# The last normalisation of a batch moves from VectorE to ScalarE, in a two-layer graph network kernel run from step lists

## The chip, the core and the metric

The kernel runs on one core of a Trainium2 chip. The core's engines each work through a queue of their own: TensorE (PE in the profile; PEld is its weight load), VectorE (DVE), ScalarE (ACT), GpSimd (POOL), and SyncE (SP), whose queue issues nearly all DMAs. They meet only at semaphores. The metric is the device time in microseconds of one execution; lower is better.

## The reference

Everything is float32. For each of 128 batches there are 128 agents with 512 features and an adjacency matrix. Layer 0 is attention with 8 heads, masked by the adjacency, and layer 1 a graph attention; each is followed by a residual and a layer norm.

```python
# layer 0
q, k, v = (x @ W + b for W, b in ((Wq, bq), (Wk, bk), (Wv, bv)))
logits = where(adj > 0, einsum('bqhd,bkhd->bhqk', q, k) / sqrt(64), -1e9)
out = relu(einsum('bhqk,bkhd->bqhd', softmax(logits), v) @ Wo + bo)
x = layernorm(x + out)
# layer 1
Wh = x @ W
e = where(adj > 0, leaky((Wh @ a1)[:, :, None] + (Wh @ a2)[:, None, :]), -9e15)
out = leaky(einsum('bij,bjf->bif', softmax(e, axis=1), Wh))
x = layernorm(x + out)            # the result: 128 x 128 x 512
```

`layernorm` is `(x - mean) / sqrt(var + 1e-5)` over the 512 features, without learned scale or offset. The normalisation that the change touches is the one in the last line.

## The kernel before

Four batches make a group. The products with Wq, Wk and Wv are made for a group at a time by Strassen's scheme, twice nested. Each of the three has two chains (numbered 0 to 5 within a group: Q, Q, K, K, V, V), and a chain has seven steps p1 to p7. A step in an even chain has 4 matrix products of 128x128x128, in an odd chain 3; the profile shows two MATMUL records for each, so 8 and 6. This document calls them group steps and writes "3.4's p2" for step p2 of chain 4 of group 3. The products with Wo (layer 0's output, `LayerZero`) and with layer 1's W (`LayerOne`) are made for pairs of batches, with seven products of 4 records each.

Each engine runs its instructions in the order in which the program emits them. That order is written out: `BEGIN` holds the tokens for the first six batches, `PLAN` those for the end, and `STEADY` has four lists, for batch t with t % 4 = 0, 1, 2, 3. A loop over t from 6 to 123 walks through the lists. An even t starts a pair and works on `LayerOne` of an earlier pair; an odd t works on `LayerZero` of the pair before. A token is a job and a method:

- `f` and `s`: softmax of the pair's first and second batch. `scores` are TensorE's (L872), `add` and `reduce` VectorE's (L886, L895), `exp` and `divide` ScalarE's, one instruction a head (L906, L920). Then `store` writes the weights to DRAM (L927), `fetch` reads them back in 4 pieces by blocks of 32 (L933), `transpose` turns them on VectorE (L939), and `attend` is TensorE's product with V (L952).
- `w`: layer 1's product of a pair (p1 to p7, L798), `z`: layer 0's output of a pair; `g`: normalised rows of layer 0 on the way back through DRAM, `g.transpose` turns them (L423); `p.sum`, `s.sum`, `m.sum`: sums of blocks on GpSimd.
- `e`: edge attention of one batch: `turn_blocks`, `add`, `maxima`, `exp`, `divide`, `product` (L1207), `copy` (L1214). `v`: its senders, through DRAM (L1248, L1258).
- `n`: the end of the batch before. `residual` (L1217), `stats` (L1000, L1002), `rstd` (GpSimd, L1006 and L1008), `apply`, `store` (L1230).
- `h`: the next group step on TensorE. `a` and `d`: the next of its reads of PSUM on ScalarE and VectorE. `k`: the next addition of a chain's blocks on GpSimd, `k.v` the same on VectorE (L728). `i.s1a` to `i.s4b`: inner sums of the features (L497), on GpSimd, or with `.v` on VectorE. `q`: the next load of weights on SP's queue (L631), into a ring of 4 buffers. `m`: loads, masks and turns of the inputs; `m.x_one` and `m.x_pair` load features (L418).

The norm's `apply` has two forms:

```python
if self.on_scalar:
    nc.scalar.activation(self.src, self.src, AF.Identity, bias=self.shift, scale=self.r)
    return
nc.vector.tensor_scalar(
    self.src, self.src, self.mv[:, 0:1], self.r, ALU.subtract, ALU.mult)
```

Before the change the steady lists use the second (L1021). The first (L1017) is used in PLAN alone, for 8 of the last 12 results (that of batch 116 and seven more) and for six rows of layer 0; there `rstd` makes the offset by two GpSimd instructions (L1011, L1013). PSUM gives five banks to scores, products and attention values in turn, and three to the group steps.

Of the kernel before, what the change touches and what calls it, by code (L numbers as in the profile page):

```python
# [8 lines left out]
F32 = mybir.dt.float32  # L9
# [3 lines left out]
ALU = mybir.AluOpType  # L13
# [56 lines left out]

STEADY = {
    0: """
        m.masks m.sum.0 f.scores m.sum.1 m.sum.2 k.v m.turn n.residual k.v g.apply.0
        s.scores w.p1 g.store.0 q g.fetch_both w.p5 f.add.1 f.add.0 f.reduce s.add.0 s.add.1
        e.turn_blocks q w.t0 w.p6 h q m.residuals f.exp.2.3 f.exp.0.1 h w.p2 h w.t2 e.add
        f.reciprocals.0 f.exp.4.5 f.exp.6.7 a d n.stats f.reciprocals.1 w.c11 e.maxima d
        w.p7 f.divide.0.1 f.divide.6.7 a w.t3 e.exp s.reduce h h f.divide.2.3 a f.divide.4.5
        m.sum.3 n.rstd e.divide i.s1b.v d w.c22 n.apply i.s1a w.p4 h n.store f.store s.exp.2
        w.c21 m.cast v.senders h s.exp.5 a v.store w.p3 s.exp.0.1 s.exp.3.4 h h e.product
        i.s2a.v k.v g.transpose.0 g.transpose.1 s.reciprocals.0 m.x_pair k f.fetch v.fetch a  # L80
        s.exp.6.7 s.divide.2 d m.mask i.s3a.v w.c12 d i.s2b e.copy i.s3b.v
    """,
    1: """
        z.by m.cast n.residual z.p2 s.reciprocals.1 k.v n.stats p.sum.0 i.s4a h h h z.p1 h a
        a d k.v h s.divide.0.1 s.divide.3.4 s.divide.5.6 s.divide.7 z.t0 h z.p6 z.bw a z.t2
        m.turn k.v h d f.transpose z.c11 e.turn_blocks z.p7 a z.p5 d z.t3 z.c22 s.store z.p4
        q e.add k k e.maxima m.mask s.fetch z.p3 h h p.sum.1 i.s4b n.rstd h n.apply e.exp a
        e.divide z.c12 z.c21 a e.product h z.stats.1 d n.store f.attend q q m.x_one
        s.transpose z.rstd.1 p.sum.2 s.attend z.stats.0 e.copy k.v z.apply.1 f.copy z.rstd.0
        s.copy s.sum.0 k k s.sum.2 p.sum.3 s.sum.1 z.store.1 s.sum.3  # L90
    """,
    2: """
        n.residual f.scores g.apply.0 e.turn_blocks s.scores w.p1 e.add w.p2 f.add.1 f.add.0
        e.maxima f.reduce w.t0 e.exp g.store.0 m.masks q m.residuals w.p6 f.exp.6.7 w.p5
        w.t2 f.exp.4.5 f.exp.0.1 w.p7 n.stats m.turn k.v f.reciprocals.1 k.v k.v w.c11 w.t3
        h h f.exp.2.3 a w.p4 f.reciprocals.0 w.c22 d h h f.divide.4.5 n.rstd n.apply
        e.divide w.c21 v.senders g.fetch_both m.x_one n.store w.p3 f.divide.6.7 s.add.0 a d
        s.add.1 g.transpose.1 w.c12 s.reduce g.transpose.0 h e.product h f.divide.2.3 m.cast
        f.divide.0.1 a a h h v.store q f.store e.copy d m.mask v.fetch
    """,  # L100
    3: """
        m.turn n.residual k.v k z.by z.bw s.exp.3.4 a z.p1 h s.exp.2 s.exp.5 z.t0 s.exp.0.1
        s.exp.6.7 d n.stats e.turn_blocks s.reciprocals.1 q h z.p6 a d s.reciprocals.0 h
        z.p5 h z.t2 s.divide.5.6 s.divide.7 h z.p7 s.divide.0.1 s.divide.3.4 f.fetch d
        f.transpose s.divide.2 a a q q s.store q q h m.cast z.t3 e.add h z.p4 h a k p.sum.0
        n.rstd p.sum.2 h z.p2 z.c22 k n.apply k.v d z.c21 e.maxima h z.p3 a e.exp a z.c11 d
        z.stats.1 e.divide z.c12 h h e.product h h s.fetch f.attend n.store k p.sum.1 k
        z.rstd.1 d z.apply.1 q q z.store.1 q m.x_one z.stats.0 s.transpose s.attend a e.copy
        f.copy s.copy a k k z.rstd.0 s.sum.0 p.sum.3 s.sum.2 s.sum.1 m.mask s.sum.3
    """,  # L110
}

# [53 lines left out]
def kernel(  # L166
# [18 lines left out]
    nc = tc.nc  # L185
    B, P, D = x.shape
# [9 lines left out]
    small = ctx.enter_context(tc.tile_pool(name="small", bufs=3))  # L196
# [795 lines left out]
    class Norm:  # L992


        def __init__(self, src, on_scalar=False):
            self.src, self.on_scalar = src, on_scalar

        def stats(self):
            st = small.tile([P, 6], F32, name="st", bufs=4)
            nc.vector.bn_stats(st, self.src)  # L1000
            self.mv = small.tile([P, 2], F32, name="mv", bufs=4)
            nc.vector.bn_aggr(self.mv, st)  # L1002

        def rstd(self):
            ve = small.tile([P, 1], F32, name="ve", bufs=4)
            nc.gpsimd.tensor_scalar_add(ve, self.mv[:, 1:2], EPS)  # L1006
            self.r = small.tile([P, 1], F32, name="rstd", bufs=4)
            nc.gpsimd.tensor_tensor(self.r, ve, mhalf, ALU.pow)  # L1008
            if self.on_scalar:
                minus = small.tile([P, 1], F32, name="minus", bufs=4)  # L1010
                nc.gpsimd.tensor_scalar_mul(minus, self.mv[:, 0:1], -1.0)  # L1011
                self.shift = small.tile([P, 1], F32, name="shift", bufs=4)
                nc.gpsimd.tensor_tensor(self.shift, minus, self.r, ALU.mult)  # L1013

        def apply(self):
            if self.on_scalar:
                nc.scalar.activation(  # L1017
                    self.src, self.src, AF.Identity, bias=self.shift, scale=self.r
                )
                return  # L1020
            nc.vector.tensor_scalar(  # L1021
                self.src, self.src, self.mv[:, 0:1], self.r, ALU.subtract, ALU.mult
            )
# [129 lines left out]
    class Edge:  # L1153
# [12 lines left out]
        e = None  # L1166
# [55 lines left out]

        def rstd(self):
            self.norm.rstd()

        def apply(self):
            self.norm.apply()
# [295 lines left out]
    for token in BEGIN.split():  # L1523
        if token[0] in "ig" and token[1] in "12":
            g = int(token[1])
# [44 lines left out]
    for t in range(6, END):  # L1570
# [11 lines left out]
        g = (t + 3) // GROUP  # L1582
# [169 lines left out]
```

## Time and profile before

| what | value |
|---|---|
| median of 3 runs | 2266.84 us (2261.54 to 2272.79) |
| the profiled execution, its own time | 2263.41 us |
| its span, first to last instruction | 2261.6 us |
| granted TensorE clock | 0.998 |
| PE, PEld, DVE, ACT, POOL busy | 2236.6, 2015.0, 2014.3, 1661.6, 1406.2 us |
| DMA | 540.78 MB, mean 239 GB/s |

The span has three stages: BEGIN until about 132 us, the loop with the STEADY lists until about 2142 us, and PLAN. In a row of the profile the columns are line, engine, operation, output<-input with shapes, count, then busy time in us and the mean of one in ns, then the idle time before them and what ended it. In a row of the chain of waits the columns are start, length and what ran. TensorE's ends are modelled, so the distance between starts is read for its steps.

### The profile page before, as it was taken

What the parts mean: (1) busy time and instruction counts of PE and PEld (TensorE: products, weight loads), DVE (VectorE), ACT (ScalarE), POOL (GpSimd) and SP (SyncE); (2) the same over time, 40 slices, a digit from 0 to 9 for tenths busy, and PEclk for the clock granted to TensorE, in tenths of its full rate; (3) what the DMA queues carried; (4) which work ended last, traced back from release to release, by engine and by line L of the source; (5) the groups of instructions that cost most, each with busy time, mean ns of one, the idle gap of its engine ahead of it and who ended that gap; (6) DMA issues with size and microseconds to landing.
All of it is one profiled execution on the core that took longest, in us unless ns stands there. A gap on an engine that the chain in (4) does not pass through costs nothing.

```text
span 2261.6 us, 52550 instructions
## 1 busy us (share of the span) xinstructions
PE 2236.6 (99%) x17228; PEld 2015.0 (89%) x17228; DVE 2014.3 (89%) x4225; ACT 1661.6 (73%) x5955; POOL 1406.2 (62%) x1697
## 2 busy tenths in 40 slices
PE   9899999999999999999999999999999999999998
PEld 6889999999999999999899999999999999999985
DVE  5889999999988999988999889999899988899977
ACT  3668777677677787776776777877767767778786
POOL 2666666656766566666567665666665676556656
PEclk9999999999999999999999999999999999999999
DMA  9988788887888888888888888888888888888764
GB/s 230 273 238 239 237 245 248 240 249 231 243 244 250 247 239 239 241 247 242 235 237 245 241 249 246 239 239 246 244 241 247 235 243 239 250 247 237 219 214 151
DMA packets 516592, 540.78 MB, mean 239 GB/s; under 512 B 100568, under 2 KB 394336, under 8 KB 516320
## 3 DMA queue, kind: packets, MB, share of 16 engines
q1 hardware_dynamic: 516000, 537.17, 81.3%
q8 instruction: 137, 2.24, 0.4%
q14 instruction: 135, 1.11, 0.2%
q10 hardware_dynamic: 320, 0.26, 0.0%
HBM read 388.96 MB, written 148.31 MB: 238 GB/s over the span
## 4 chain that ended last, share of the span: by engine, by line
PE 89%; DMA 4%; DVE 4%; ACT 1%; SPq 1%; issue 1%; POOL 0%; POOLq 0%; DVEq 0%; ACTq 0%
PE st_y L678 24%; PE p_y L798 19%; PE st_w L678 12%; PE p_w L798 9%; PE st_x L678 6%; PE lg L872 6%; PE p_oT L952 5%; PE p_x L798 5%; PE p_h L1207 4%; DMA adj<-in_adj_dram 1%; DMA paz<-pa_dram 1%; DMA w_n<-wv 0%; SPq L933 0%; ACT pa L920 0%; DVE pa L939 0%
## 5 line engine op out<-in xcount | busy, mean ns | idle before, releaser
L906 ACT ACTIVATE pa<-pa,nmax 128x128 f32<-128x128 f32 x1000 | 391.8, 397 | 11.7 <-DVE nmax L895 9.4
L920 ACT ACTIVATE pa<-pa,rs 128x128 f32<-128x128 f32 x1000 | 327.2, 401 | 4.1 <-DVE rs L916 4.1
L728 POOL TENSOR_TENSOR out_Q<-out_Q,cells 128x512 f32<-128x512 f32 x92 | 116.2, 1277 | 297.4 <-DVE out_Q L728 297.4
L691 ACT COPY cells<-st_y 128x384 f32<-128x384 f32 x279 | 133.0, 477 | 102.6 <-PE st_y L678 101.9
L967 ACT ACTIVATE arena<-p_oT,b_cols 128x128 f32<-128x128 f32 x504 | 138.1, 382 | 80.6 <-PE p_oT L952 79.7
L906 ACT ACTIVATION_READ_ACCUMULATOR pa<-pa,nmax 128x1 f32 x1000 | 193.4, 193 | 0.0
L1008 POOL TENSOR_TENSOR rstd<-ve,mhalf 128x1 f32<-128x1 f32 x256 | 161.4, 631 | 21.3
L1000 DVE BATCH_NORM_STATS2 st<-arena 128x6 f32<-128x512 f32 x248 | 168.8, 681 | 1.2
L1006 POOL TENSOR_SCALAR ve<-mv 128x1 f32<-128x1 f32 x256 | 76.1, 297 | 147.7 <-DVE mv L1002 145.0
L886 DVE TENSOR_TENSOR pa<-lg,mf 128x512 f32<-128x512 f32 x250 | 161.5, 675 | 3.7 <-PE lg L872 3.7
L939 DVE STREAM_TRANSPOSE pa<-paz 128x1024 f32<-128x1024 f32 x125 | 154.6, 1236 | 7.0 <-DMA w_n<-wv 3.0
L895 DVE TENSOR_REDUCE nmax<-pa 128x8 f32<-128x1024 f32 x125 | 151.0, 1208 | 1.2
L872 PE MATMUL lg<-out_K,out_Q 64*128 64x128 f32 x2048 | 139.6, 281 | 0.7 <-ACT out_K L1391 0.7
L872 PEld LDWEIGHTS lg<-out_K,out_Q 64*128 64x128 f32 x2048 | 125.2, 187 | 14.3 <-issue 7.2
L728 POOL TENSOR_TENSOR out_K<-out_K 128x512 f32<-128x512 f32 x62 | 79.1, 1275 | 91.1 <-DVE out_K L728 91.1
L712 DVE TENSOR_TENSOR cells<-st_w,cells 128x384 f32<-128x384 f32 (+1 forms) x217 | 120.9, 557 | 16.6 <-ACT cells L691 16.3
L798 PE MATMUL p_y<-wo_w,x1T 128*128 128x257 f32 x496 | 134.2, 393 | 0.0
L1214 ACT ACTIVATE arena<-p_h 128x512 f32<-128x512 f32 x120 | 71.9, 599 | 83.8 <-DMA out_dram<-arena 60.2
L798 PE MATMUL p_y<-wo_w,arena 128*128 128x256 f32 x504 | 131.3, 383 | 0.9 <-ACT pr_t L809 0.9
L1021 DVE TENSOR_SCALAR arena<-arena,mv,rstd 128x512 f32<-128x512 f32 x239 | 131.2, 549 | 0.6 <-POOL rstd L1008 0.6
L798 PE MATMUL p_y<-wo_w,oS 128*128 128x256 f32 x504 | 129.8, 380 | 0.1
L798 PE MATMUL p_y<-wo_w,x1S 128*128 128x257 f32 x496 | 128.2, 380 | 0.2 <-ACT arena L809 0.2
(301 smaller groups left out, 7720.8 us busy)
## 6 DMA issues: line engine op xcount, KB each, us to landing
paz<-pa_dram SPq DMA_DIRECT2D x504, 128.0 KB, 3.6
pa_dram<-pa SPq DMA_DIRECT2D x125, 512.0 KB, 3.8
w_n<-wk SPq DMA_DIRECT2D x93, 512.0 KB, 4.3
w_n<-wv SPq DMA_DIRECT2D x93, 512.0 KB, 5.1
w_n<-wk SPq DMA_DIRECT2D x93, 384.0 KB, 4.3
w_n<-wv SPq DMA_DIRECT2D x93, 384.0 KB, 3.5
x_dram<-arena SPq DMA_DIRECT2D x128, 256.0 KB, 2.6
xz<-x_dram SPq DMA_DIRECT2D x240, 128.0 KB, 3.8
```

Source lines behind the costliest of these rows:

```text
L678: nc.tensor.matmul(p[:, index, :], lhs, rhs, start=start and index == 0, stop=True, skip_group_check=True,)
L728: (by or engine).tensor_add(*(t(n) for t, n in (dst, left, right)))
L798: nc.tensor.matmul(p[:, :width], xs()[n][:, kc, :], w[:, PLACE[n], kc, :], start=start and kc == 0, stop=True, skip_group_check=True,)
L872: nc.tensor.matmul(self.lg[r][:, c, :], q[rows, 2 * (b % 2) + c % 2, c // 2, :], k[rows, 2 * (b % 2) + c % 2, c // 2, :], start=c == 0, st ...
L886: nc.vector.tensor_add(by_head[:, r * NC : (r + 1) * NC], self.lg[r].rearrange("p c (b k) -> p c b k", b=4), mf.unsqueeze(1).to_broadcast( ...
L895: nc.vector.tensor_reduce(self.nmax, by_head, AX.XY, ALU.max, negate=True)
L906: nc.scalar.activation(self.pa[:, :, h, :], self.pa[:, :, h, :], AF.Exp, bias=self.nmax[:, h : h + 1], accum_out=self.sums[:, h : h + 1],)
L920: nc.scalar.activation(self.pa[:, :, h, :], self.pa[:, :, h, :], AF.Copy, scale=self.rs[:, h : h + 1])
L939: nc.vector.transpose(self.paT.rearrange("p h (a i) -> p a h i", i=32), self.paz.rearrange("p a (h k) -> p a h k", k=32),)
L967: nc.scalar.activation(OT[pair][:, c, h * P : (h + 1) * P], self.oT[:, c, :], AF.Identity, bias=b_cols[:, 1, c : c + 1],)
L1000: nc.vector.bn_stats(st, self.src)
L1008: nc.gpsimd.tensor_tensor(self.r, ve, mhalf, ALU.pow)
```

## The change

`Edge` gets a token `move`. It makes the offset, -mean x rstd, by one VectorE instruction on 128x1 values and sets `on_scalar`, so that the `apply` which follows is ScalarE's. As `on_scalar` is set after `rstd` has run, GpSimd's two offset instructions are not emitted. All four STEADY lists have `n.move` added and are reordered throughout; BEGIN and PLAN are the same text.

```diff
+        def move(self):
+
+            self.shift = small.tile([P, 1], F32, name="shift", bufs=4)
+            nc.vector.scalar_tensor_tensor(
+                self.shift, self.mv[:, 0:1], -1.0, self.r, op0=ALU.mult, op1=ALU.mult
+            )
+            self.on_scalar = True
...
+        def move(self):
+            self.norm.move()
```

Of the lists, the parts that the prediction speaks of. The new list 0, from its start and around the weights' way:

```
m.sum.0 m.sum.1 m.sum.2 e.turn_blocks m.turn f.scores k.v n.residual m.masks k.v
g.apply.0 q f.add.0 f.add.1 s.scores w.p1 f.reduce a e.add w.t0 m.cast n.stats
m.mask g.store.0 n.rstd h f.exp.4.5 f.exp.2.3 m.sum.3 e.maxima w.p6 w.t2 f.exp.0.1
s.add.0 d s.add.1 f.reciprocals.0 h q m.residuals g.fetch_both a e.exp f.exp.6.7
f.divide.0.1 d s.reduce f.reciprocals.1 q q q w.p2 w.p7 h h w.p5 h a w.t3 a s.exp.5
f.divide.6.7 w.p4 n.move w.c22 i.s1b.v d w.c11 w.p3 h h e.divide g.transpose.1
g.transpose.0 n.apply f.divide.2.3 i.s1a w.c21 v.senders f.divide.4.5 n.store
s.exp.6.7 a v.store f.store h e.product h s.exp.3.4 s.exp.0.1 s.exp.2 a d k.v
m.x_pair i.s3b.v s.reciprocals.0 s.reciprocals.1 w.c12 d v.fetch i.s2a e.copy
f.fetch i.s3a i.s2b
```

The old list 0 from e.divide on:

```
e.divide i.s1b.v d w.c22 n.apply i.s1a w.p4 h n.store f.store s.exp.2
w.c21 m.cast v.senders h s.exp.5 a v.store w.p3 s.exp.0.1 s.exp.3.4 h h e.product
i.s2a.v k.v g.transpose.0 g.transpose.1 s.reciprocals.0 m.x_pair k f.fetch v.fetch a
s.exp.6.7 s.divide.2 d m.mask i.s3a.v w.c12 d i.s2b e.copy i.s3b.v
```

The new list 1:

```
z.p2 k p.sum.0 p.sum.2 h h s.divide.3.4 z.by a h z.p1 h h h n.residual n.stats k.v a
d s.divide.2 s.divide.0.1 s.divide.7 s.divide.5.6 k.v m.turn e.turn_blocks z.bw z.t0
a k.v z.p6 z.t2 z.p5 i.s4b k z.p7 n.rstd k i.s4a h f.transpose n.move s.store d z.t3
e.add e.maxima z.c22 a e.exp m.cast n.apply z.p4 h z.c21 e.divide h z.p3 d z.c11
z.stats.1 z.c12 q s.fetch h h e.product a a n.store d s.transpose z.stats.0 f.attend
z.rstd.1 q s.attend z.apply.1 e.copy p.sum.1 k k m.x_one f.copy s.copy z.rstd.0
s.sum.0 s.sum.2 s.sum.1 p.sum.3 k s.sum.3 m.mask z.store.1
```

Counted over the four lists, `h` goes from 9, 11, 8, 14 to 9, 11, 5, 17 (lists 0 to 3) and `q` from 3, 3, 2, 8 to 5, 2, 2, 7; `i.s2a` and `i.s3a` lose their `.v`; of the additions 13 instead of 12 are GpSimd's and 11 instead of 12 VectorE's.

## The prediction

> **What bounds the kernel now.** I read the page's busy line first, then busy time by stage, TensorE's waits, and the chain that ended last inside the steady stage.
>
> ```profile
> PE 2236.6 (99%) x17228; PEld 2015.0 (89%) x17228; DVE 2014.3 (89%) x4225; ACT 1661.6 (73%) x5955; POOL 1406.2 (62%) x1697
> ```
>
> ```profile
> 0.00:132.00 132.00, 121.08 (x777) 95.15 (x777) 96.50 (x186) 72.42 (x248) 69.38 (x67) 0.99 0.89 245
> 132.00:2142.00 2010.00, 2007.50 (x15767) 1830.64 (x15764) 1825.16 (x3828) 1497.72 (x5404) 1265.87 (x1512) 1.00 0.83 242
> 2142.00:2262.00 120.00, 108.06 (x690) 89.19 (x688) 92.66 (x213) 91.50 (x305) 70.97 (x120) 0.98 0.59 184
> ```
>
> The columns are PE, PEld, DVE, ACT, POOL, clock, DMA. The second row is the loop that uses the changed lists: TensorE (PE) idles 2.5 of 2010 us, VectorE (DVE) 185. The first and third rows are BEGIN and PLAN, which the change leaves alone; they hold 22.8 of the 25 us that TensorE idles.
>
> A busy TensorE could still be a slow one, so I looked at the length of its steps:
>
> ```profile
> 236.61 2.29 PE lg L872 x31
> ```
>
> ```profile
> 253.82 1.56 PE st_y L678 x14
> 260.46 0.89 PE st_y L678 x8
> 264.85 1.56 PE st_y L678 x14
> 267.30 0.86 PE p_h L1207 x2
> 268.83 1.90 PE p_oT L952 x32
> 270.73 1.99 PE lg L872 x32
> 272.71 1.06 PE p_y L798 x4
> ```
>
> 1.56/14 and 0.89/8 are both 0.111 us a matmul: a group step of 8 or 6 matmuls takes 0.89 or 0.67, wherever it stands. Only the scores (lg) differ: 1.99 in list 2, up to 2.29 in list 0. Starts of the scores of successive pairs are 34.90 and 34.08 us apart, 68.98 for four batches. The rows give: 21 steps of 8 and 21 of 6, 32.8; 28 products of 0.866, 24.2, and 0.2 more for each of the two behind the scores, 0.4; 4 products of 0.86, 3.4; attention values and scores of two pairs, 2x1.90 + 2x1.99 = 7.8. Sum 68.6. So one round of four lists has 0.3 to 0.4 us of give, some 10 us in the 29.5 rounds.
>
> Here a rule of the Trainium skill is weighed: "Perfetto Trace Analysis", section "Identifying the Most-Contended Engine", says that matmul busy time is a bad measure of TensorE's headroom and that LDWEIGHTS' busy share is a good one. By that rule 89% leaves 11%, 247 us, to be won. By the equal steps it is 10 us in the lists. I take the steps: nothing but the waits between them can go.
>
> **The change part by part.**
>
> The apply. 116 steady results (128 less the last 12, whose norm lies in PLAN) go from VectorE to ScalarE (ACT):
>
> ```profile
> L1021 DVE TENSOR_SCALAR arena<-arena,mv,rstd 128x512 f32<-128x512 f32 x239 | 131.2, 549 | 0.6 <-POOL rstd L1008 0.6
> L1017 ACT ACTIVATE arena<-arena,shift,rstd 128x512 f32<-128x512 f32 x9 | 7.3, 813 | 2.5 <-POOL shift L1013 2.3
> L1201 DVE RECIPROCAL rt<-total 128x1 f32<-128x1 f32 x128 | 19.6, 153 | 6.5 <-ACT att L1197 4.8 <-ACT wq L1197 1.5
> ```
>
> VectorE loses 116 x 0.549 = 63.7 us. The new offset instruction is 128x1; the trace has no 128x1 scalar_tensor_tensor. Nearest are this reciprocal (0.153) and the 128x2 aggregate L1002 (0.182); the 128x1 additions L394 had a median of 0.278, in a stage with queueing. I take 0.18: 20.9 us, between 18 and 32. ScalarE gains 116 x 0.813 = 94.3 us. The rule that speaks against this is in "ScalarE: Activation LUTs", section "Rules for kernel authors": additions and multiplications belong on VectorE, not ScalarE. Were both engines in series with TensorE, it would make the change 116 x (0.813 + 0.18 - 0.549) = +51.5 us. In the trace neither is: ScalarE has 512 us free in the loop. I put the direct cost at 0; the cover is TensorE's 68.6 us a round against about 51 of ScalarE, and if it failed wholly the price would be those 51.5.
>
> The lists. I summed each engine's instructions per round, each at the distance between starts that the trace shows when it runs back to back. VectorE goes from 61.3 to 58.2 us: apply and offset, and two sums of features (i.s2a, i.s3a: rows of 0.678 and 1.279, L497) that go to GpSimd. ScalarE goes from 48.7 to 51.5. GpSimd (POOL) goes from 42.1 to 45.3: it takes the two sums at 1.80 and 1.28. All stay under 68.6. On the page I expect VectorE near 1915 us, ScalarE 1755, GpSimd 1495, and TensorE unchanged: it has the same steps, the group steps in the same order among themselves; list 2 has 5 group steps instead of 8 and list 3 has 17 instead of 14. The DMAs are the same ones; only their places in the SP queue move. By themselves these moves cost 0: every sum stays covered.
>
> What a new order can win. In list 0 the second scores wait: K's last addition (k.v, L728) ran 236.82 to 237.50 on VectorE and the scores could have begun at 237.53; with their semaphore instructions they started at 237.64. The blocks of scores in list 0 are 0.14 to 0.48 over the 1.99 (mean 0.24), 7.3 us in all. In the new lists VectorE ends s's turn 1.7 us before list 0 begins (in list 3 its last waits are for p3 of 3.3, 4.6 us ahead; then 0.47 + 0.59 + 1.16 and what stood before); the turned edges 0.23, an addition 0.59, the residual 0.60 and K's last addition 0.59 then end 0.3 us into the list, 0.7 before the second scores at 0.99. Part of the 0.24 is the sequencer's own work, so I count -5 us (bounds 0 and -7). Short stalls at 1074 to 1094 cost 2.4 us once; with VectorE freer I count -1.
>
> What it can cost: queues. Places in a list are TensorE's steps added up from its first scores: w.p3 of the new list 0 ends at 2 scores 1.99 + 7 products 6.06 + 4 group steps of 8 and one of 6, 4.24 = 12.3. n.store waits in SP's queue for the apply on ScalarE; behind it stand v.store and f.store in lists 0 and 2, weight loads (q) and z.store in 1 and 3. ScalarE has the apply, some 0.72 at back-to-back spacing, ahead of two divisions of f in list 0. There five q now come before n.store; the last waits for a weight buffer that the Q/K/V step p3 frees at 10.6 us into the list, before the apply ends at 11.3: 0. n.move waits for GpSimd's rstd and holds VectorE's queue (w.c22, i.s1b, an addition). rstd stands behind three feature sums of 1.24; the first began 4.9 us into the old list 0, so rstd ends at 4.9 + 3.7 + 0.8 = 9.4. The first TensorE step that reads a bank which the held addition must empty (3.5's p2) starts at 13.65, the addition ends by 11.3: room of 2 us. On GpSimd list 1 has 17.0 us of work in 17.8; i.s4a, the last sum before the second Q chain, ends at 25.4 from list 0's start (i.s4b from 19.3: 0.96, two V additions of 1.24, rstd 0.82, i.s4a 1.83), its reader starts at 26.9: room of 1.5. The tightest place is list 1's turn:
>
> ```profile
> 249.79 0.38 SPq L927 DMA_DIRECT2D pa_dram<-pa  x1
> 252.13 1.82 SPq L418 DMA_DIRECT2D xz<-in_x_dram  x4
> 254.04 2.58 SPq L933 DMA_DIRECT2D paz<-pa_dram  x4
> 256.66 2.02 SPq L1258 DMA_DIRECT2D ez<-e_dram  x4
> ```
>
> ```profile
> 260.99 1.23 DVE L939 STREAM_TRANSPOSE pa<-paz 128x1024 f32<-128x1024 f32 x1
> 268.18 1.23 DVE L939 STREAM_TRANSPOSE pa<-paz 128x1024 f32<-128x1024 f32 x1
> ```
>
> The weights of head block f are stored (L927), fetched (L933) and turned (L939) on VectorE, then those of s; s is used by the second half of the 268.83 row, at 269.78, and turned at 269.41. Room: 0.37 us. In the new order the x loads (L418) can go 1.7 us earlier (their buffers are freed after w.p3, which ends 12.3 us into the list instead of 14.0), but v.fetch (L1258, 2.02 us of issue) now stands before f.fetch. So f.fetch begins about 0.3 us later, +17.8 instead of +17.5 into list 0, its last piece is down 6.4 to 6.8 us later (24.2 to 24.6), and VectorE, which had no idle time before this turn, waits for it some 1.6 us. From there to the end of s's turn the new list has 8.2 us on VectorE (the old one took 8.42): 32.4 to 32.8. The s product starts at 32.69. I put half of the win back: +2.
>
> Sum against the profiled execution's own time, 2263.4 (span 2261.6 and 1.8 around it): -5 - 1 + 2 = -4, 2259.4. The median shown, 2266.84, lies 3.4 above that execution, so I round up to 2260.
>
> **The rivals.**
>
> Slower: a late turn in list 1. Each 0.1 us that f's fetch lands later than 24.6 delays s's product by as much, 29 times: 2.9 us. It decides from 0.6 us: 18 us, 2278; at 1 us it gives 29 us, 2289. For it: the room above is nil by my sums, n.apply stands ahead of f.store and v.store, and v.fetch must wait for v.store's landing (3.0 us before). Against it: the x loads come earlier, and VectorE's own share is shorter.
>
> No change: TensorE's 68.6 us a round hid everything before and hides it now; the waits at the scores only change place. 2263 to 2267.
>
> Faster by more: all of the list's give and most of the small stalls go, and executions like the slower two of the three shown had more such stalls, which a freer VectorE absorbs. 2261.6 + 1.8 - 7.3 - 2.5 = 2253.6; nothing in the lists can give more.
>
> Doing nothing is not possible for the instructions, but it is for the time: that is the second case.
>
> **How the numbers follow.** 0.5% is 11.3 us, about what a measurement of this kernel can tell from no change: below 2255.5 is faster, above 2278.2 slower. The forecast (2255.5 to 2266) has 0.38, no change 0.08, the late turn 0.30 (0.05 of it too small to count as slower), more gain 0.18, all of it below 2255.5, other new waits, in an order whose rooms are about 0.5 us, 0.06 (slower). So faster 0.18, same 0.38 + 0.08 + 0.05 = 0.51, slower 0.25 + 0.06 = 0.31. The range takes in most of the larger gain, to 2252, and the late turn up to 0.9 us, 2286; some 0.05 lies below and 0.1 above.
>
> **What would show it.** Right: TensorE's loop still within 3 us of full, VectorE's share near 85%, ScalarE's near 78%, scores of list 0 at 2.0 to 2.1 us, 116 more applies on ScalarE at about 0.81 us. Wrong: idle time of TensorE at p_oT ended by VectorE's turn (L939) and the turn idle until DMA paz, above 0.3 us in every fourth list; or group steps (L678) waiting for VectorE's additions. A time outside 2252 to 2286 or a TensorE with fewer idle microseconds in BEGIN and PLAN would mean that I read the bound wrongly.

## The result: slower by 1.6%, and the profile after

The changed kernel takes 2304.09 us (2296.92 to 2306.25, 5 runs) against 2266.84 before (2261.54 to 2272.79): ratio 1.0161, 95% interval 1.0143 to 1.0179, 37 us. The forecast was 2260 and its range ended at 2286. The profiled execution took 2305.97 us, span 2304.2, granted clock 0.999.

Line numbers after are those of before plus 2 up to the norm, plus 10 behind it and plus 13 from `Edge.move` on (L678 is L680, L939 is L941, L1008 is L1018, L1021 is L1031, L1258 is L1271); the offset is L1003.

First the page's busy line and the busy time by stage (columns as before: PE, PEld, DVE, ACT, POOL, clock, DMA share, GB/s):

```profile
PE 2260.2 (98%) x17228; PEld 2007.4 (87%) x17228; DVE 2009.4 (87%) x4138; ACT 1724.0 (75%) x6071; POOL 1515.7 (66%) x1784
```

```profile
0.00:132.00 132.00, 119.36 (x779) 93.07 (x779) 96.98 (x187) 71.91 (x248) 69.53 (x67) 1.00 0.87 247
132.00:2182.00 2050.00, 2030.36 (x15754) 1823.08 (x15752) 1817.38 (x3735) 1557.85 (x5509) 1375.63 (x1597) 1.00 0.82 237
2182.00:2304.00 122.00, 110.45 (x700) 91.25 (x699) 95.06 (x218) 94.26 (x314) 70.53 (x122) 0.98 0.60 186
```

The loop is 40 us longer and holds nearly the whole loss; in it TensorE idles 20 us instead of 2.5. (The other half hides in "busy": a matmul whose start is held shows in the distance between starts and not always as idle.) VectorE was to fall to about 1915 us and stands at 2009.4, as before: the work taken off it came back in longer instructions. The chain that ended last tells the same in one line; before it was 89% TensorE:

```profile
PE 39%; DVE 25%; ACT 12%; DMA 8%; POOL 7%; SPq 5%; issue 4%; DVEq 0%; POOLq 0%; ACTq 0%
```

Next the groups of instructions that the change touched, and under them the tile view of the offset (ns min/median/max):

```profile
L1027 ACT ACTIVATE arena<-arena,shift,rstd 128x512 f32<-128x512 f32 x125 | 101.9, 815 | 2.5 <-POOL shift L1023 2.3
L1031 DVE TENSOR_SCALAR arena<-arena,mv,rstd 128x512 f32<-128x512 f32 x123 | 91.0, 740 | 14.0 <-POOL rstd L1018 14.0
L1003 DVE SCALAR_TENSOR_TENSOR shift<-mv,rstd 128x1 f32<-128x1 f32 x116 | 51.5, 444 | 3.1 <-POOL rstd L1018 3.1
L1018 POOL TENSOR_TENSOR rstd<-ve,mhalf 128x1 f32<-128x1 f32 x256 | 189.2, 739 | 21.3
```

```profile
L1003 DVE SCALAR_TENSOR_TENSOR shift<-mv,rstd x116: 116/144/1225, 176.4 to 2204.4; 128x1 f32<-128x1 f32 x116
```

ScalarE's apply is as sized (815 ns for 813). The offset is not: 444 ns in the mean for 180, though half of them take 144 or less. The applies that stayed on VectorE went from 549 to 740 ns, and now they idle 14.0 us for GpSimd's rstd instead of 0.6; rstd itself went from 631 to 739.

TensorE's waits, as the view of waits gives them:

```profile
PE p_oT L954 <- DVE pa L941: 10.5, 13, 1.8
PE p_y L800 <- ACT arena L811: 7.3, 29, 0.3
...
PE st_w L680 <- DMA w_n<-wv: 1.8, 5, 0.6
```

Neither the first nor the second was there before above 2 us. To place them I took the distances between starts of successive pairs' first scores, 29 of each kind. Lists 2 and 3 together went from 34.98 to 36.30 us in the mean, lists 0 and 1 from 34.15 to 34.28: 38 us of the loss are in lists 2 and 3, 4 in 0 and 1. Then every gap between neighbouring matmuls was set against its usual length. By place, in us over the 29 rounds:

| place | waits for | after | before |
|---|---|---|---|
| A list 2, w.p4 | ScalarE's read of w.t3 (L811) | 15 | 0 |
| B list 3, s.attend (p_oT) | VectorE's turn of s's weights (L941) | 11.7 | 1.2 |
| C list 2, w.p5 | f.add on VectorE, which empties a bank (L888) | 8.3 | 0.1 |
| D list 3, group step behind e.product | its weights (DMA w_n) | 4.6 | 0 |
| E list 1, second Q chain | GpSimd's i.s4a (L499) | 4.5 | 0 |
| list 1, s.attend (p_oT) | VectorE's turn | 0.7 | 0 |

The last row is the place where the prediction had looked for a late turn. Its rows, after:

```profile
251.55 0.32 SPq L929 DMA_DIRECT2D pa_dram<-pa  x1
251.97 2.43 SPq L420 DMA_DIRECT2D xz<-in_x_dram  x4
254.49 1.88 SPq L1271 DMA_DIRECT2D ez<-e_dram  x4
256.41 1.96 SPq L935 DMA_DIRECT2D paz<-pa_dram  x4
...
262.06 1.23 DVE L941 STREAM_TRANSPOSE pa<-paz 128x1024 f32<-128x1024 f32 x1
269.43 1.24 DVE L941 STREAM_TRANSPOSE pa<-paz 128x1024 f32<-128x1024 f32 x1
269.91 1.97 PE L954 MATMUL p_oT<-pa,out_V 128*64 128x128 f32 x32
```

v.fetch (L1271) now stands before f.fetch, which begins 18.9 us into list 0 (17.5 before), and still s's turn ends at 270.67, before its half of p_oT at 270.86.

A and C come from one place, the start of list 2 (scores at 271.81). VectorE first, then GpSimd:

```profile
269.43 1.24 DVE L941 STREAM_TRANSPOSE pa<-paz 128x1024 f32<-128x1024 f32 x1
270.59 0.66 DVE L1010 BATCH_NORM_STATS2 st<-arena 128x6 f32<-128x512 f32 x1
...
271.91 0.31 DVE L1193 STREAM_TRANSPOSE e_turned<-ez 128x128 f32<-128x128 f32 x1
272.14 0.65 DVE L1227 TENSOR_TENSOR arena<-arena 128x512 f32<-128x512 f32 x1
273.25 1.06 DVE L1031 TENSOR_SCALAR arena<-arena,mv,rstd 128x512 f32<-128x512 f32 x1 [0.46 <-POOL rstd L1018]
274.24 1.28 DVE L888 TENSOR_TENSOR pa<-lg,mf 128x512 f32<-128x512 f32 x2
```

```profile
272.12 1.10 POOL L1018 TENSOR_TENSOR rstd<-ve,mhalf 128x1 f32<-128x1 f32 x1
273.30 0.73 POOL L522 TENSOR_TENSOR oS<-arena 128x256 f32<-128x256 f32 x1
273.99 0.91 POOL L524 TENSOR_TENSOR oS<-arena 128x256 f32<-128x256 f32 x1
```

Behind s's turn VectorE still has z.stats.0 and z.apply.1 of list 1, a mask, the turned edges and the residual; then g.apply.0 waits 0.46 us for rstd, which takes 1.10 beside that residual, and runs 1.06 us beside GpSimd's sums: it ends at 274.31, 0.28 us after the first of them (274.03). f's additions start 2.4 us behind f's scores, the exps 5.1. w.t3 stands behind those exps on ScalarE, and w.p4 behind w.t3.

### The profile page after: what moved, and what is told of

It reads as the page before. It is cut to its first block, busy times and chain, and to the rows that moved or that the text cites. A ratio compares the mean times of both kernels' runs of the same rounds, so it can differ in the third digit from the quotient of the medians.

```text
span 2304.2 us, 52613 instructions
## 1 busy us (share of the span) xinstructions
PE 2260.2 (98%) x17228; PEld 2007.4 (87%) x17228; DVE 2009.4 (87%) x4138; ACT 1724.0 (75%) x6071; POOL 1515.7 (66%) x1784
## 3 DMA queue, kind: packets, MB, share of 16 engines
q8 instruction: 137, 2.24, 0.4%
q14 instruction: 135, 1.11, 0.2%
## 4 chain that ended last, share of the span: by engine, by line
PE 39%; DVE 25%; ACT 12%; DMA 8%; POOL 7%; SPq 5%; issue 4%; DVEq 0%; POOLq 0%; ACTq 0%
PE st_y L680 12%; PE p_y L800 8%; PE st_w L680 6%; DMA paz<-pa_dram 4%; ACT pa L908 4%; PE p_w L800 4%; DVE pa L941 3%; POOL rstd L1018 3%; DVE pa L888 3%; PE st_x L680 3%; DVE arena L1031 2%; ACT pa L922 2%; DVE nmax L897 2%; DVE st L1010 2%; PE p_x L800 2%
## 5 line engine op out<-in xcount | busy, mean ns | idle before, releaser
L1018 POOL TENSOR_TENSOR rstd<-ve,mhalf 128x1 f32<-128x1 f32 x256 | 189.2, 739 | 21.3
L908 ACT ACTIVATION_READ_ACCUMULATOR pa<-pa,nmax 128x1 f32 x1000 | 198.8, 199 | 0.0
L730 POOL TENSOR_TENSOR out_K<-out_K 128x512 f32<-128x512 f32 x62 | 91.9, 1483 | 141.8 <-DVE out_K L730 141.8
L941 DVE STREAM_TRANSPOSE pa<-paz 128x1024 f32<-128x1024 f32 x125 | 154.6, 1236 | 20.6 <-DMA w_n<-wv 10.5
L888 DVE TENSOR_TENSOR pa<-lg,mf 128x512 f32<-128x512 f32 x250 | 163.0, 672 | 4.1 <-PE lg L874 4.0
L954 PEld LDWEIGHTS p_oT<-pa,out_V 128*64 128x64 f32 x2000 | 107.2, 136 | 44.3 <-issue 23.1
L954 PE MATMUL p_oT<-pa,out_V 128*64 128x128 f32 x2000 | 128.8, 277 | 11.0 <-DVE pa L941 10.5
L1016 POOL TENSOR_SCALAR ve<-mv 128x1 f32<-128x1 f32 x256 | 70.2, 274 | 102.7 <-DVE mv L1012 101.0
L811 ACT COPY arena<-p_y 128x257 f32<-128x257 f32 x184 | 67.6, 367 | 83.8 <-PE p_y L800 83.8
```

Source lines behind the costliest of these rows:

```text
L730: (by or engine).tensor_add(*(t(n) for t, n in (dst, left, right)))
L888: nc.vector.tensor_add(by_head[:, r * NC : (r + 1) * NC], self.lg[r].rearrange("p c (b k) -> p c b k", b=4), mf.unsqueeze(1).to_broadcast( ...
L908: nc.scalar.activation(self.pa[:, :, h, :], self.pa[:, :, h, :], AF.Exp, bias=self.nmax[:, h : h + 1], accum_out=self.sums[:, h : h + 1],)
L941: nc.vector.transpose(self.paT.rearrange("p h (a i) -> p a h i", i=32), self.paz.rearrange("p a (h k) -> p a h k", k=32),)
L954: nc.tensor.matmul(self.oT[r * HD : (r + 1) * HD, c, :], v[:, c % 2, c // 2, r * HD : (r + 1) * HD], self.paT[:, r * NC + c, :], start=c == 0,
```

## Experiments

All are compared with the kernel before on the same chip; its median there was 2265.4 to 2268.4.

### Is it the engine or the order?

Old lists with n.move put directly ahead of n.apply, so that ScalarE applies:

```diff
-        m.sum.3 n.rstd e.divide i.s1b.v d w.c22 n.apply i.s1a w.p4 h n.store f.store s.exp.2
+        m.sum.3 n.rstd e.divide i.s1b.v d w.c22 n.move n.apply i.s1a w.p4 h n.store f.store s.exp.2
```

(so in all four lists.)

> The old step lists, with n.move put just ahead of n.apply in each, so that only the apply changes engine. Order theory (the new lists lose the 40 us, the engine change is harmless): ratio to before 0.996 to 1.004, TensorE idle in the loop below 5 us, VectorE busy some 45 us less than before, ScalarE some 95 us more. Engine theory (0.8 us more in ScalarE's queue, and its store behind it, delays softmax and stores in any order): 1.008 to 1.018, with new waits of TensorE on ScalarE's copies or on turned weights. If both share the loss it lies between 1.004 and 1.008.

Measured: 2331.5 us, ratio 1.0289 (1.0271 to 1.0308).

New lists with n.move taken out of all four, so that VectorE applies:

```diff
-        f.divide.6.7 w.p4 n.move w.c22 i.s1b.v d w.c11 w.p3 h h e.divide g.transpose.1
+        f.divide.6.7 w.p4 w.c22 i.s1b.v d w.c11 w.p3 h h e.divide g.transpose.1
```

> The new step lists without n.move, so that the apply stays on VectorE at its new place. Order theory: ratio 1.012 to 1.024, with the same waits as in the changed kernel (w.p4 on ScalarE's copy in list 2, w.p5 on VectorE's addition of the mask, s's attention product on the turn), a little more where VectorE carries the apply. Engine theory: 0.997 to 1.006.

Measured: 2376.5 us, ratio 1.0488 (1.0468 to 1.0508). Against the kernel before, in us:

| | VectorE applies | ScalarE applies |
|---|---|---|
| old lists | 0 | +65 |
| new lists | +110 | +37 |

Both theories fall: each of the two runs lies outside both of its expected ranges. The move of the work costs 65 us in the old lists and brings 72 in the new ones; the lists cost 110 with one engine and bring 27 with the other. So the new lists do what they were searched for: they take back 27 of the 65. In the old lists ScalarE is what TensorE waits for, from the waits of the first kernel:

```profile
PE st_y L678 <- ACT cells L691: 33.8, 58, 1.2
PE p_oT L952 <- DVE pa L939: 16.4, 32, 1.3
```

L691 is the read (`a`) of a group step's bank; it stands behind the apply in ScalarE's queue in lists 0 and 2. The turn of list 1 is late for a third such place. The apply stands directly ahead of e.exp there, and VectorE idles at e.divide until e.exp is done, ahead of s's turn. One round, ScalarE first and then VectorE:

```profile
266.80 0.81 ACT L1025 ACTIVATE arena<-arena,shift,rstd 128x512 f32<-128x512 f32 x1 [1.48 <-DVE shift L1001]
```

```profile
268.03 0.16 DVE L1209 RECIPROCAL rt<-total 128x1 f32<-128x1 f32 x1 [1.27 <-ACT att L1205]
```

That idle time is 1.26 to 1.27 us in each of the 29 rounds, and none before the change; VectorE never idles directly ahead of this turn, so the fetched weights are there in time.

In the second kernel the apply's own row shows a likely part of the 110:

```profile
L1031 DVE TENSOR_SCALAR arena<-arena,mv,rstd 128x512 f32<-128x512 f32 x239 | 198.0, 829 | 14.1 <-POOL rstd L1018 14.1
```

829 ns instead of 549, 67 us more for the same 239 instructions; how much of it TensorE felt, no run took apart. Only their neighbours on the other engines are different: 120 of them took 0.51 to 0.57 us, the other 119 took 0.88 to 1.32, and of these 118 ended 0.28 to 0.29 us after the end of a GpSimd addition that was at work when they began or began with them.

### Can single tokens mend it?

In the changed kernel, list 2, g.apply.0 goes behind f's maxima:

```diff
-        e.turn_blocks f.scores e.add n.residual g.apply.0 f.add.1 f.add.0 e.maxima s.scores
-        w.p1 w.t0 e.exp f.reduce m.turn n.stats k.v w.p5 w.p6 k.v k h h f.exp.0.1 w.t2
+        e.turn_blocks f.scores e.add n.residual f.add.1 f.add.0 e.maxima s.scores
+        w.p1 w.t0 e.exp f.reduce g.apply.0 m.turn n.stats k.v w.p5 w.p6 k.v k h h f.exp.0.1 w.t2
```

> The changed kernel with one token moved in list 2: g.apply.0 behind f.reduce instead of ahead of f.add.1. In the changed kernel it waits 0.46 us for GpSimd's rstd and takes 1.06 us on VectorE, and f.add, f.reduce, f.exp and w.t3 follow it. If that is what makes w.p5 and w.p4 late in list 2 (8 and 15 us of stalls), both stalls go and the ratio falls from 1.016 to about 1.005 to 1.008. If ScalarE is late by its own load there, w.p4's stall stays: 1.011 to 1.014.

Measured: 2318.7 us, ratio 1.0222 (1.0195 to 1.0249), slower than the changed kernel and outside both expected ranges. A's wait fell from 15 to 8 us, C's went, and B's fell too (by some 8 of 11.7 us); but waits grew that take 0.3 and 1.5 us in the changed kernel:

```profile
PE st_y L680 <- DVE out_K L714: 6.2, 10, 1.5
PE st_w L680 <- DVE cells L714: 5.8, 4, 2.0
```

The same with s.reduce earlier in list 2, in m.mask's place:

```diff
-        f.store a m.mask d v.fetch g.transpose.0 g.transpose.1 e.copy s.reduce w.c12
+        f.store a s.reduce d v.fetch g.transpose.0 g.transpose.1 e.copy m.mask w.c12
```

> As the kernel with g.apply.0 late, and in list 2 s.reduce also moved ahead of the two g.transpose, in the place of m.mask, which goes to the list's end. In the changed kernel VectorE waits 1.0 us there for ScalarE's cast of the mask and then 0.1 us for w.p3, and s's exponentials wait for s.reduce. If the stall of s's attention product in list 3 (12 us) starts there, it goes too: ratio 0.999 to 1.004. If it comes from the store and fetch queue alone, it stays, and the ratio is that of the kernel with g.apply.0 late, within 0.002.

Measured: 2319.6 us, ratio 1.0239 (1.0212 to 1.0266): no gain, so s.reduce's place was not what made B. g.apply.0 has something queued on it too (g.store, g.fetch_both, the turns and sums made from it). Most of the new waits stand in list 3; that they come from its delay is read from the lists, no run showed it.

In the old lists with ScalarE's apply, the apply goes behind the reads that waited for it, and n.store behind f.store and v.store:

```diff
-        w.c22 n.move n.apply i.s1a w.p4 h n.store f.store s.exp.2
-        w.c21 m.cast v.senders h s.exp.5 a v.store w.p3
+        w.c22 n.move i.s1a w.p4 h f.store s.exp.2
+        w.c21 m.cast v.senders h s.exp.5 a n.apply v.store n.store w.p3
...
-        f.divide.4.5 n.rstd n.move n.apply
-        e.divide w.c21 v.senders g.fetch_both m.x_one n.store w.p3 f.divide.6.7 s.add.0 a d
+        f.divide.4.5 n.rstd n.move
+        e.divide w.c21 v.senders g.fetch_both m.x_one w.p3 f.divide.6.7 s.add.0 a n.apply n.store d
```

> Old lists with the apply on ScalarE, as in the first experiment (2331.5 us), but in lists 0 and 2 n.apply stands one to three tokens later, behind the read (a) of the next group step's bank, and n.store behind f.store and v.store; n.move stays. In the first experiment TensorE lost 23.2 + 2.6 us in list 0 and 17.1 + 2.8 in list 2 at group steps that waited for such a read, and 18.5 in list 1 at the second p_oT, whose turn was late because f.store had stood behind n.store. Theory 'places': the loss belongs to what is queued behind the apply, so these 64 us go nearly whole: 2262 to 2280 us, p_oT in list 1 within 3 us of waiting in all. Theory 'work': 0.81 us a batch has no free place on ScalarE in lists whose rooms are a few tenths of a microsecond, so the reads' wait only moves to the divisions and exps: above 2300 us.

Measured: 2322.0 us, ratio 1.0249 (1.0224 to 1.0274), 9.5 less than without these moves. The time lies in the range of the theory "work", but the run shows less than that theory:

```profile
PE p_oT L952 <- DVE pa L939: 15.8, 31, 1.3
PE st_w L678 <- ACT cells L691: 8.8, 29, 0.4
PE st_w L678 <- ACT out_K L691: 3.8, 9, 0.7
```

In list 0 the reads came free: some 26 us of waiting there became 2, with some 7 new in list 1. In list 2 the waits moved on to the next read (the second row). The turn of list 1 (the first row) waits as long as before, because only lists 0 and 2 were changed: in list 1 the apply still stands ahead of e.exp, and VectorE idles the same 1.27 us. The theory that f.store behind n.store made this turn late falls: f.store went out 12.0 instead of 13.8 us into list 0, and f.fetch began at 17.6 in both kernels and in the kernel before. A better place for list 1's apply was not tried.

### What the apply costs, and what the lists cost

The old lists without n.apply (n.rstd stays):

```diff
-        m.sum.3 n.rstd e.divide i.s1b.v d w.c22 n.apply i.s1a w.p4 h n.store f.store s.exp.2
+        m.sum.3 n.rstd e.divide i.s1b.v d w.c22 i.s1a w.p4 h n.store f.store s.exp.2
```

> Old lists, and the last normalisation of the 116 steady batches is left out altogether (no apply on any engine; statistics and rstd stay). VectorE loses 63 us of work and nothing is added. It bounds what taking the apply off VectorE can bring at most. If TensorE's equal steps are the bound: 2255 to 2267 us, no more than 0.5% below the kernel before. If VectorE's load held TensorE up somewhere that I did not see: below 2250.

Measured: 2261.5 us, ratio 0.9986 (0.9976 to 0.9995). So 64 us of work less on VectorE (116 x 0.549) were worth about 3 us (1 to 5 by the interval): there was next to nothing to win by relieving it. The new lists without n.move and n.apply:

```diff
-        f.divide.6.7 w.p4 n.move w.c22 i.s1b.v d w.c11 w.p3 h h e.divide g.transpose.1
-        g.transpose.0 n.apply f.divide.2.3 i.s1a w.c21 v.senders f.divide.4.5 n.store
+        f.divide.6.7 w.p4 w.c22 i.s1b.v d w.c11 w.p3 h h e.divide g.transpose.1
+        g.transpose.0 f.divide.2.3 i.s1a w.c21 v.senders f.divide.4.5 n.store
```

> New lists, and the last normalisation of the 116 steady batches is left out (neither offset nor apply on any engine). ScalarE loses 94 us of work against the changed kernel, VectorE the 51 us that the offset took. Theory 'lists': the stalls come from the new places at the start of list 2 (VectorE's backlog behind s's turn, g.apply's wait for GpSimd and its double length beside GpSimd) and of the late turn in list 3, and stay: 2285 to 2300 us. Theory 'ScalarE': without its 0.81 us a batch the reads and exps come in time: 2272 or less.

Measured: 2296.2 us, ratio 1.0128 (1.0107 to 1.0150). The new lists alone cost 29 to 31 of the 37 us. A, B and C are all there: 14.9, 7.6 and 7.5 us. Lists 2 and 3 take 36.07 us a pair, lists 0 and 1 34.12. The apply and its offset add 8 us to that.

### Why VectorE's instructions are longer

In the changed kernel 58 of the 116 offsets ran while GpSimd was idle and took 0.13 us in the mean (0.12 to 0.14). The other 58 began while GpSimd was in one of its additions; 54 of them took 0.43 to 1.22. All 58 ended 0.01 to 0.02 us after the end of that addition, as here (389.19 and 389.17; VectorE first, then GpSimd):

```profile
388.36 0.83 DVE L1003 SCALAR_TENSOR_TENSOR shift<-mv,rstd 128x1 f32<-128x1 f32 x1
```

```profile
387.90 1.27 POOL L525 TENSOR_TENSOR xT<-xT,xS 128x512 f32<-128x512 f32 x1
```

The offset has two tensor inputs in SBUF. The Trainium skill, "SBUF — State Buffer", section "Who interferes with whom", says that VectorE's second read port is shared with GpSimd and locked for a whole instruction, that a VectorE instruction with two SBUF inputs needs it against a GpSimd instruction that reads SBUF, and that the one that comes second waits. To test it here, the same value was made from one tensor input:

```diff
-                nc.vector.scalar_tensor_tensor(
-                    self.shift, self.mv[:, 0:1], -1.0, self.r, op0=ALU.mult, op1=ALU.mult
-                )
+                nc.vector.tensor_scalar(
+                    self.shift, self.mv[:, 0:1], self.r, -1.0, ALU.mult, ALU.mult
+                )
```

> The changed kernel, the same tokens in the same order; only the offset is made by a tensor_scalar with rstd as its scalar operand (one tensor input) instead of a scalar_tensor_tensor with two. In the changed kernel the offset took 0.13 us where GpSimd was idle and 0.43 to 1.22 us beside GpSimd's work, 51.5 us in all instead of the 21 that I had taken. Theory 'shared port' (two inputs in SBUF are what makes it wait for GpSimd): each offset takes 0.12 to 0.2 us also beside GpSimd, VectorE's busy time falls by 25 to 35 us, and the time by up to that, 2275 to 2298 us, if the backlog behind the offset is what delays the exps and turns. If the length comes from something else (it is recorded while it waits for rstd), it stays near 0.44 us and the time within 3 us of 2304.

Measured: 2291.2 us, ratio 1.0105 (1.0084 to 1.0127), 13 us less than the changed kernel with every token at its place.

Its tile view, and its row among the groups:

```profile
L1003 DVE TENSOR_SCALAR shift<-mv,rstd x116: 166/174/215, 176.6 to 2186.0; 128x1 f32<-128x1 f32 x116
```

```profile
L1003 DVE TENSOR_SCALAR shift<-mv,rstd 128x1 f32<-128x1 f32 x116 | 21.3, 184 | 4.3 <-POOL rstd L1018 4.3
```

The longest fell from 1225 to 215 ns, with 58 of the 116 beside GpSimd's work again, and VectorE's busy time from 2009.4 to 1971.3 us. The rule holds for the offset.

How the 13 us came about is in part luck. At the start of list 2 VectorE's g.apply.0 waits for GpSimd's rstd, and GpSimd's next sum follows that rstd, so that the two begin nearly together. In the changed kernel they began within 0.06 us of each other, and g.apply.0 took 0.94 to 1.07. In 15 of 29 rounds it now began 0.14 us ahead of the sum and took 0.55 us (one of them, VectorE and GpSimd):

```profile
273.21 0.55 DVE L1031 TENSOR_SCALAR arena<-arena,mv,rstd 128x512 f32<-128x512 f32 x1 [0.46 <-POOL rstd L1018]
```

```profile
273.35 0.99 POOL L522 TENSOR_TENSOR oS<-arena 128x256 f32<-128x256 f32 x1 [0.17 <-ACT arena L969]
```

In these rounds TensorE began the group step behind w.p4 8.87 us into list 2. In the other 14 the sum was ahead by 0.05 to 0.06, g.apply.0 took 0.94 to 0.96, and that step began at 9.43, as in the changed kernel (9.46). 15 times 0.56 is 8.4 us, all of what A and C fell by. With no offset at all the sum was ahead in every round, and A and C stayed. So the wait of the two-input offset is shown, but the 13 us are what shortening it set off here, and not its price. This kernel beats the new lists without any apply (2296.2 us) by 5 us, less than these 8.4; without them ScalarE's apply and the short offset would cost some 3 us, an estimate from these two runs.

### What is left: the starts of list 2 and of list 3

On top of that, g.apply.0 of list 2 runs on ScalarE, with GpSimd making its offset:

```diff
-            self.norms[h] = Norm(X1[2 * self.pair + h], self.on_scalar)
+            on_scalar = self.on_scalar or (h == 0 and self.late)
+            self.norms[h] = Norm(X1[2 * self.pair + h], on_scalar)
...
             jobs = {"z": LayerZero((t - 3) // 2), "p": jobs["g"]}
+            jobs["z"].late = t % GROUP == 1
```

> The previous experiment's kernel (offset with one tensor input, 2291.2 us), and in list 2 g.apply.0 stays at its place in the lists but runs on ScalarE, its offset made by GpSimd behind rstd; ScalarE is idle there for 1.5 us. VectorE no longer waits 0.46 us for GpSimd's rstd and does not run 0.55 us of g.apply ahead of f's additions. Theory 'backlog at the start of list 2': f's additions, maxima and exps come 0.9 to 1.0 us earlier; TensorE's waits for w.t3 at w.p4 (7.9 + 3.0 us) and for f's addition at w.p5 (2.3 + 1.6) go: 2274 to 2280 us. Rival: the start of f's exps is not what w.t3 waits for (it has its own place behind other ScalarE work): 2288 us or more.

Measured: 2280.5 us, ratio 1.0060 (1.0043 to 1.0078), 10.7 less, half a microsecond above the range of the first theory and far from the rival's. f's additions start 1.21 us into list 2 instead of 2.09 in the mean, the exps 3.85 instead of 4.72. A fell from 10.9 to 4.2 us and C from 3.9 to nothing: that is as much as the whole gain. The backlog on VectorE at the start of list 2, with g.apply.0 in it, is shown as the cause of C and of most of A.

List 3 next: an earlier s.store by another order of ScalarE's divisions.

```diff
-        s.divide.5.6 a
-        e.turn_blocks s.reciprocals.0 d d s.divide.0.1 e.add s.divide.3.4 s.divide.2 z.c11
-        e.maxima m.turn s.divide.7 z.t2
+        s.divide.5.6
+        e.turn_blocks s.reciprocals.0 s.divide.0.1 a d d s.divide.3.4 s.divide.2 z.c11
+        s.divide.7 e.add e.maxima m.turn z.t2
```

> The kernel just before, and in list 3 ScalarE's order is changed once: the read (a) that stood between the first two divisions of s waits for TensorE for 0.43 us and goes behind s.divide.0.1, and e.add (0.39) and e.maxima go behind s.divide.7. s.store then comes 0.8 us earlier, and with it in SP's queue the weight loads and s.fetch behind it. Theory 'late s.store in list 3': TensorE's waits for s's turn at p_oT (5.8 us) and for the weights behind e.product (4.6 us) go: 7 to 11 us less than the kernel just before, 2264 to 2272 us, level with the kernel before the change. Rival: the weight buffers, which come free by group steps, hold the queue and not s.store, or the moved read makes a group step wait: within 4 us of the kernel just before.

Measured: 2282.4 us, ratio 1.0068 (1.0048 to 1.0088): nothing gained, as the rival said. SP's queue shows a reason:

```profile
292.59 0.34 SPq L633 DMA_DIRECT2D w_n<-wv  x1
293.04 0.37 SPq L929 DMA_DIRECT2D pa_dram<-pa  x1
294.38 0.37 SPq L633 DMA_DIRECT2D w_n<-wk  x1
296.58 0.37 SPq L633 DMA_DIRECT2D w_n<-wv  x1
297.70 1.75 SPq L935 DMA_DIRECT2D paz<-pa_dram  x4
```

The store now goes out directly behind a weight load and takes longer to land (4.57 us in the mean for 3.93; the table below has both), and s.fetch waits for the landing. Two more runs, on the kernel with ScalarE's g.apply.0: first GpSimd's i.s4a of list 1 ahead of the addition before it,

```diff
-        n.rstd k i.s4a h f.transpose
+        n.rstd i.s4a k h f.transpose
```

> The kernel with g.apply.0 of list 2 on ScalarE (2280.5 us), and in list 1 GpSimd makes the inner sum i.s4a ahead of the chain addition (k) that stood before it, 1.2 to 1.8 us of GpSimd's work. In that kernel TensorE lost 2.3 + 1.6 + 0.9 us at the second Q chain's first step, which waits for i.s4a. Theory 'room of list 1 on GpSimd overdrawn': these 4 to 5 us go: 2274 to 2278 us. Rival: the addition that now comes later makes TensorE or V's reader wait instead: within 2 us of 2280.5.

Measured: 2298.0 us, ratio 1.0127 (1.0104 to 1.0150): 17.5 us slower, where 4 to 5 less were expected. The wait for i.s4a went; the chain addition that now comes 1.3 us later, and those behind it on GpSimd, cost 10.5 us at a group step and 6.4 at p_oT:

```profile
PE st_y L680 <- ACT cells L699: 8.4, 18, 0.7
PEld p_oT L954 <- POOL out_Q L730: 7.7, 29, 0.3
```

The second row is the weight load of p_oT, and out_Q is what such an addition writes. One exchange of two neighbours on an engine that is busy 67% moved the kernel by 0.8%. The second run has this exchange and the earlier divisions too, and lets s.store go ahead of the weight load:

```diff
-        z.t3 q q h p.sum.2 k p.sum.1 k z.p4 a m.cast s.store h d f.transpose
+        z.t3 q h p.sum.2 k p.sum.1 k z.p4 a m.cast s.store q h d f.transpose
```

> The kernel with the earlier divisions of s in list 3 (2282.4 us), with the same move of i.s4a, and in list 3 the weight load (q) that went out 0.1 us before s.store stands behind it. In the three kernels at hand s.store landed 3.8 us after its issue where the last load had gone out 1.4 us before it, 4.3 where 0.8, 4.5 where 0.1. Theory 'the store lands behind the loads': it lands 0.5 to 0.7 us sooner, s.fetch and s's turn with it, TensorE's 7.3 us of waiting at p_oT in list 3 go nearly whole, and with the 4 to 5 us of i.s4a the time is 2269 to 2275 us. Rival: the landing takes its 4.3 to 4.5 us whatever stands ahead, or the load behind it comes late for a group step: no more than i.s4a's part, 2276 to 2280 us.

Measured: 2297.0 us, ratio 1.0127 (1.0110 to 1.0144). As the exchange's 17 us are in it, the time missed both expectations, and the question is read from the trace. Means over the 29 rounds, us from list 2's first scores (s's turn: its start):

| kernel | gap before s.store | s.store | its landing | s.fetch | s's turn | waits at B |
|---|---|---|---|---|---|---|
| before | 2.07 | 21.56 | 3.76 | 25.38 | 32.45 | 1.2 |
| changed | 1.13 | 23.09 | 3.88 | 27.15 | 33.96 | 11.7 |
| g.apply.0 on ScalarE | 1.11 | 22.53 | 3.93 | 26.62 | 33.21 | 5.0 |
| and earlier divisions | 0.54 | 21.94 | 4.57 | 26.67 | 33.24 | 7.3 |
| and the load behind s.store | 1.88 | 21.71 | 4.05 | 26.00 | 33.06 | 5.3 |

The landing part holds: 4.57 to 4.05, s.fetch 0.67 earlier. The rest of the way gave most of it back: the fetch itself landed 6.6 us after its issue instead of 6.1, and the turn comes only 0.18 earlier. With the store back at 21.71, where it was before, 5.3 us of B remain: the late store is at most a part of B.

## Why the prediction was wrong, point by point

**The bound** was right. Without any apply the old lists gain 3 us. The rule that the busy share of weight loads measures TensorE's headroom (the Trainium skill, "Perfetto Trace Analysis", section "Identifying the Most-Contended Engine"; it names the FLOPs achieved beside it, which I did not take) would leave 11% here. No run found any of it: a group step took the same 0.111 us a matmul in every kernel. From this bound, taking the apply off VectorE could bring some 3 us and cost anything.

**"The lists ... by themselves these moves cost 0: every sum stays covered"** is the step that failed. The sums were of an engine over a round, and they do stay under 68.6 us. Not covered were places: the new lists alone cost some 30 us with ScalarE's apply left out. I laid out list 1's turn, and two queues besides, and did not lay out lists 2 and 3, though I had noted that three group steps move from list 2 to list 3. I had VectorE free 1.7 us before list 0 and thought of no backlog at list 2. There z.stats.0, z.apply.1 and a mask stand behind s's turn in list 1, and g.apply.0 waits for GpSimd. That is A and C. In list 3 the turn had 0.36 us of room before, in most rounds; now s.store goes out 1.5 us later and s.fetch 1.8. That goes with B: in 16 of the 18 rounds that wait, VectorE idled for a DMA ahead of the turn.

**The late turn** was therefore the right kind of mechanism in the wrong list, and "TensorE idle at p_oT ended by the turn every fourth list" is what came, for about a quarter of the loss (B). In list 1 the fetch came 1.1 us later than the 17.8 I had worked out (18.9), yet the turn was in time: 0.7 us of wait in all, for the +2 that I had taken.

**The offset** was mis-sized: 51.5 us for 20.9, above my upper bound of 32. In the old lists it takes 188 ns, as taken; in the new ones 444. I sized it by instructions that did not wait for GpSimd. The same goes for the applies left on VectorE (740 ns for 549) and for "VectorE near 1915" (2009.4). I read durations from the old order and carried them into a new one. The trace of before held a sign: 3 of its 239 applies took 0.88 to 1.09 us, at 101, 107 and 133 us, and 33 of its 256 rstd took 0.9 to 1.1. Making the offset with one input brought 13 us of the 37, 8.4 of them by the race for g.apply.0.

**ScalarE's apply at 0**, against the rule of the Trainium skill, "ScalarE: Activation LUTs", section "Rules for kernel authors", that additions and multiplications belong on VectorE: nearly right in the new lists (some 3 us with the one-input offset, by the estimate above), wrong in the old ones, where the same work at its old place cost 65 us. That this lies near the 51.5 of "both engines in series" shows nothing: the waits came from three places where something stood right behind the apply. The cover is the order, not the 17 us a round in which ScalarE is idle.

**The scores of list 0**, -5: they took 2.21 us instead of 2.24 in the mean, 0.6 us over all rounds. The reading was right, and the win did not come because VectorE was no earlier: K's addition ended 0.88 us into the list in the mean, for 0.90 before and the 0.3 forecast. In the one round in which it ended at 0.62 the scores took 1.99.

**i.s4a's room of 1.5 us** was overdrawn: it ended 27.3 us into list 0 in the mean, for 25.4 in my sum. GpSimd's instructions ahead of it were longer than in the old order: i.s4b took 0.99 to 1.46 us for the 0.96 taken, the first V addition 1.72 to 1.82 for 1.24, rstd with its addition 1.30 for 0.82. My sum also had GpSimd going through without a pause; it idles 0.76 us in the mean for VectorE's read of a bank ahead of the first V addition. i.s4a itself was shorter, 1.27 for 1.83. It cost 4.5 us (E). n.move's room and n.store's place behind five weight loads were right: no wait of TensorE names them.

**Sums.** Of the 42.6 us between the two profiled executions: A and C 23, B and D 15 (before 1), E 4.5; together 42.5. The 13 us that the one-input offset brought are inside A, B and C (they fell by 4.1, 5.9 and 4.4), not beside them. Left open: what of B and D is the later s.store and what the three group steps more in list 3 and their weights' traffic; no run took these apart. The cause of C and most of A is shown by a run; that of B and D is read from traces.

No version here beats the kernel before. The best with ScalarE's apply is 2280.5 us.

## What to carry to other kernels

Where one engine is at its floor and the rest is a hand-laid or searched order, busy shares say nothing of what a move costs: lay out every place where the bound engine waits for a buffer, not only the tightest of before, and take room from there. Ask what leaving the work out altogether would bring before moving it; here 3 us. When work moves between engines, ask of each instruction that stays what will now run beside it: for a small VectorE instruction prefer the form with one tensor input where GpSimd is at work, and ask which of two neighbours on VectorE and GpSimd will be first.

## What the runs showed of the hardware that I had not expected

A 128x1 VectorE instruction with two SBUF inputs takes 0.12 to 0.14 us when GpSimd is idle and up to 1.22 beside it: all 58 that began within a GpSimd addition ended 0.01 to 0.02 us after it. With one tensor input it takes 0.17 to 0.22 in both cases. It works both ways: GpSimd's rstd, 0.57 us at the median, takes 1.10 at places beside VectorE's residual and ends 0.43 us after it. So these two engines do not meet only at semaphores, as the opening has it.

The 128x512 apply (one tensor input, two scalars) waits too: 0.54 us alone, as much as 1.09 beside GpSimd's sums in the changed kernel and 1.32 with the new lists and VectorE's apply, where 118 of 119 long ones ended 0.28 to 0.29 us after a GpSimd addition that was at work when they began or began with them. Who is first decides: begun 0.14 us ahead of the sum, g.apply.0 took 0.55, and the sum 0.99 instead of 0.73; begun within 0.06 of it, 0.94 to 1.07. In the old lists it ran with GpSimd idle 147 times of 239, and 3 were long. Which property of this instruction makes it wait, no run told.
